# A vision tower on one core: in the expert attention, values laid out by head, their biases added by VectorE, and no gate transposes

## The chip, the cores and the metric

The kernel runs on one core of one Trainium2 chip. The metric is device time in microseconds, the median of three runs: before the change it is 2742.89 us (2742.8 to 2744.47). The core has five engines that run their own instruction streams and wait for one another by semaphores: TensorE (in the profile PE, its weight loads PEld), VectorE (DVE), ScalarE (ACT), GpSimd (POOL) and SyncE (SP, which only issues DMAs here). TensorE writes into PSUM[...]. VectorE and ScalarE empty PSUM into SBUF. Everything is in fp32.

## The reference, cut to what matters

The model is a tokenizer, two transformer layers and, in each, an attention and a feed-forward part. The change touches the feed-forward part of layer 0, which is itself an attention, one for each of 4 experts, 4 chunks of 64 features and 2 heads:

```python
gate = softmax(xn @ router_w.T + router_b, axis=-1)          # 4 gates a token
xc = xn.reshape(B, T, C, DC)                                 # B=128, T=64, C=4, DC=64
qkv = einsum('btcd,ekd->btcek', xc, qkv_w)                   # 4 experts, 2 heads of 32
attn = softmax(einsum('bcehtd,bcehsd->bcehts', q, k) * scale, axis=-1)
y = einsum('bcehts,bcehsd->bcehtd', attn, v)
y = einsum('btced,eod->btceo', y, proj_w) + proj_b           # one bias vector an expert
out = einsum('btceo,bte->btco', y, gate).reshape(B, T, D)
return residual + out @ out_w.T
```

## The kernel before, in words

The stage is the function `expert_attention`. It holds the tokens of all 128 images in SBUF (`h2`) and works on pairs of images: 64 pairs of 2 x 64 = 128 tokens. `Block` does LayerNorm, the transposes of the normalized tokens and the gates for four pairs at once; `Pair` does the attention of one pair.

The weights of values and projection are multiplied together before the loop (`wvp`, L806 to L814), so the "values" of an expert and a head have already been projected to 64 features. The softmax weights are multiplied by the gate (L991, L992 on POOL), so summing over experts and heads in PSUM (`mixed`, L1014) gives the gated output. The projection's bias is brought in apart: before the loop the kernel multiplies the biases by the output matrix (`pb`, `b4`, L819 to L821) and spreads the result by four DMAs over a zeroed tile (`bn`, L823 to L825). For each block the gates are transposed by TensorE (`gates_transpose`, L908) and copied by ScalarE (L911) into one of three zeroed tiles (`gT`, L828), and each pair's `output` adds to its two products with `wo` (L1028) a third one of `gT` with `bn` (L1029). VectorE then adds the sum to `h2` (L1030), and after every fourth pair SP writes four pairs to HBM (L1032).

The order of the work is written out by hand. `with tc.manual_schedule()` keeps each engine's instructions in program order; only what stands before it (the weights, the first blocks' LayerNorm) is ordered by the scheduler. In step p of the loop over pairs three pairs are in flight: scores and softmax of the current pair, the transposes and the mixing of the old one, queries, keys and values of the new one. TensorE's order in a step is: scores (L965), queries and keys of chunk pair 0 (L933), the old pair's second weight transposes (L1001), queries and keys of chunk pair 1, `mixed` (L1014), `values(0)` and `values(1)` (L945), `output` (L1028, L1029), the steps of a block (L908, L874 or L885), and, at the head of the next step, the first weight transposes (L1001). VectorE's order is: maxima and differences of the scores (L977, L978), sums (L984, L985), block steps (statistics L843 and L844 in two of four steps, the logits' steps L892 to L901 in a third), the copies of `values(1)` out of PSUM (L954) and the addition L1030.

`work` holds the steps of the blocks by pair number and place, so the four pairs of a block differ: with p modulo 4, step 0 has a gate transpose and four token transposes on TensorE; step 1 four token transposes, and statistics on VectorE; step 2 the logits, and statistics; step 3 the logits' softmax on VectorE and none of these on TensorE.

All PSUM tiles but the scores come from one pool of four banks with the tag `pq`. A new tile takes the bank that was released longest ago, and its first matmul waits for that bank's last reader.

In `values(fc)`, four 64x64 parts of TensorE's array are used at once: row half `par`, column half `eh`. One call covers two of the four chunks and all 256 columns of `wvp`; its two banks (one for each `par`) are copied by ScalarE for `fc` 0 and by VectorE for `fc` 1.

Of the kernel before, what the change touches and what calls it, by code (L numbers as in the profile page):

```python
# [11 lines left out]
F32 = mybir.dt.float32  # L12
# [7 lines left out]
P = 128  # L20
B = 128
T = 64
D = 256
# [737 lines left out]
def expert_attention(c, hd, normw, wr, br, wqkv, wvT, wproj, bproj, wout):  # L761
# [3 lines left out]
    tc, nc, h2 = c.tc, c.nc, c.h2  # L765
    SCALE = float(1.0 / np.sqrt(np.float32(32)))
    NP = B // 2
    NB = 4
    with (
# [12 lines left out]
        brs = wp.tile([P, 4], F32, name="brs")  # L782
        nc.sync.dma_start(brs, br.partition_broadcast(P))
        w = wp.tile([P, 2 * D], F32, name="w")
        bp2 = wp.tile([P, 4], F32, name="bp2")
        for k in range(2):
            nc.sync.dma_start(w[k * 64 : k * 64 + 64, :], wqkv)
            nc.sync.dma_start(bp2[k * 64 : k * 64 + 64, :], bproj)
        wv = wp.tile([32, 8, 64], F32, name="wv")
        nc.scalar.dma_start(wv, wvT)  # L790
        wpj = wp.tile([32, 8, 64], F32, name="wpj")
# [10 lines left out]
        for k in range(2):  # L802
            for e in range(4):
                for h in range(2):
                    r = (e % 2 * 2 + h) * 64
                    nc.tensor.matmul(  # L806
                        pv[k * 64 : k * 64 + 64, e // 2, r : r + 64],
                        wv[:, e * 2 + h, :],
                        wpj[:, e * 2 + h, :],
                        start=True,  # L810
                        stop=True,
                    )
        wvp = wp.tile([P, 2, D], F32, name="wvp")
        nc.vector.tensor_copy(wvp, pv)  # L814


        pb = psq.tile([4, D], F32, tag="pq", name="pb")
        for fc in range(2):
            nc.tensor.matmul(pb, bp2, wo[:, fc, :], start=(fc == 0), stop=(fc == 1))  # L819
        b4 = wp.tile([4, D], F32, name="b4")  # L820
        nc.vector.tensor_copy(b4, pb)  # L821
        bn = wp.tile([P, NB, D], F32, name="bn")
        nc.gpsimd.memset(bn, 0.0)  # L823
        for n in range(NB):
            nc.sync.dma_start(bn[4 * n : 4 * n + 4, n, :], b4)  # L825
        gTs = [wp.tile([P, P], F32, name=f"gT{k}") for k in range(3)]
        for gT in gTs:
            nc.gpsimd.memset(gT, 0.0)  # L828

        class Block:  # L830

            def __init__(self, p0):
                self.p0, self.gT = p0, gTs[p0 // NB % 3]

            def statistics(self, n0):
                if n0 == 0:
# [63 lines left out]
            def gates(self):  # L903
                nc.gpsimd.tensor_mul(self.gate, self.gate, bcast(self.gm, 2, 4))

            def gates_transpose(self):
                self.pgt = psq.tile([4 * NB, P], F32, tag="pq", name="pgt")
                nc.tensor.transpose(self.pgt, self.gate.rearrange("p n e -> p (n e)"), c.ident)  # L908

            def gates_transposed(self):  # L910
                nc.scalar.copy(self.gT[0 : 4 * NB, :], self.pgt)  # L911

        class Pair:


            def __init__(self, p, blk):
                self.p, self.n, self.blk = p, p % NB, blk
                self.xT = blk.xT[:, :, p % NB, :]
                self.e, self.sm, self.pT = {}, {}, {}

                self.qk = vp.tile([P, 4, 2, 2, P], F32, tag="qk", name="qk", bufs=2)

                self.v = vp.tile([P, 4, 2, D], F32, tag="v", name="v")

            def queries_keys(self, fc):

# [9 lines left out]
                for par in range(2):  # L936
                    nc.scalar.copy(self.qk[:, 2 * fc + par], pq[par])  # L937

            def values(self, fc):
                pv = [psq.tile([P, 2, D], F32, tag="pq", name="pv") for _ in range(2)]  # L940
                for j in range(2):
                    for eh in range(2):
                        for par in range(2):
                            r = slice(par * 64, par * 64 + 64)
                            nc.tensor.matmul(  # L945
                                pv[par][eh * 64 : eh * 64 + 64, j, :],
                                self.xT[r, fc, j * 64 : j * 64 + 64],
                                wvp[r, eh, :],
                                start=True,
                                stop=True,  # L950
                            )
                for par in range(2):
                    copy = nc.scalar.copy if fc == 0 else nc.vector.tensor_copy
                    copy(self.v[:, 2 * fc + par], pv[par])  # L954

            def scores(self):

# [48 lines left out]
            def mixed(self):  # L1006

                pz = psq.tile([P, 2, P], F32, tag="pq", name="pz")
                for fc in range(2):
                    for j in range(2):  # L1010
                        t = slice(j * 64, j * 64 + 64)
                        for r in range(4):
                            for par in range(2):
                                nc.tensor.matmul(  # L1014
                                    pz[par * 64 : par * 64 + 64, fc, t],
                                    self.v[:, 2 * fc + par, j, r * 64 : r * 64 + 64],
                                    self.pT[r // 2][:, r % 2, 2 * fc + par, t],
                                    start=(r == 0),
                                    stop=(r == 3),
                                )  # L1020
                self.z = ep.tile([P, 2, P], F32, tag="z", name="z", bufs=2)
                nc.scalar.copy(self.z, pz)  # L1022

            def output(self):
                p = self.p
                po = psq.tile([P, D], F32, tag="pq", name="po")
                for fc in range(2):
                    nc.tensor.matmul(po, self.z[:, fc], wo[:, fc, :], start=(fc == 0), stop=False)  # L1028
                nc.tensor.matmul(po, self.blk.gT, bn[:, self.n, :], start=False, stop=True)  # L1029
                nc.vector.tensor_add(h2[:, p], h2[:, p], po)  # L1030
                if p % 4 == 3:
                    nc.sync.dma_start(  # L1032
                        hd[2 * p - 6 : 2 * p + 2].rearrange("(n b) t f -> (b t) n f", b=2),
                        h2[:, p - 3 : p + 1],
                    )
# [5 lines left out]
        def at(n, place, f, *a):  # L1041
            key = (n, place) if n >= 0 else "first"
            work.setdefault(key, []).append(lambda: f(*a))

        for b, x in enumerate(blocks):
            n = NB * b
            at(n - 11, "DVE", x.statistics, 0)
            at(n - 10, "DVE", x.statistics, 2)
            at(n - 9, "POOL", x.factors)
            for k in range(NB):  # L1050
                at(n - 8 + k, "POOL", x.normal, k)
            at(n - 4, "PE", x.transpose, 0)
            at(n - 3, "ACT", x.transposed, 0)
            at(n - 3, "PE", x.transpose, 1)
            at(n - 2, "ACT", x.transposed, 1)
            at(n - 2, "PE", x.logits)
            at(n - 1, "DVE", x.logits_less_max)
            at(n - 1, "ACT2", x.exponents)
            at(n - 1, "DVE2", x.sums)
            at(n - 1, "POOL", x.gates)  # L1060
            at(n, "PE", x.gates_transpose)
            at(n + 1, "ACT", x.gates_transposed)

        def do(key):
            for step in work.pop(key, ()):
# [3 lines left out]
        with tc.manual_schedule():  # L1069
            old, cur = None, Pair(0, blocks[0])  # L1070
            for fc in range(2):
                cur.queries_keys(fc)
                cur.values(fc)
            for p in range(NP):
                new = Pair(p + 1, blocks[(p + 1) // NB]) if p + 1 < NP else None
                do((p, "ACT"))
                if old:
                    old.transposed(0)
                cur.scores()
                cur.less_max(0)  # L1080
                cur.less_max(1)
                if new:
                    new.queries_keys(0)
                if old:
                    old.transposed(1)
                cur.exponents(0)
                if new:
                    new.queries_keys(1)
                cur.exponents(1)
                cur.sums(0)  # L1090
                cur.weights(0)
                do((p, "DVE"))
                do((p, "ACT2"))
                cur.sums(1)
                cur.weights(1)
                do((p, "DVE2"))
                do((p, "POOL"))
                if old:
                    old.mixed()
                if new:  # L1100
                    new.values(0)
                    new.values(1)
                if old:
                    old.output()
                do((p, "PE"))
                old, cur = cur, new
            for x in range(2):
                old.transposed(x)
            old.mixed()
            do((NP, "ACT"))  # L1110
            old.output()
        assert not work

# [873 lines left out]
def layout(**i):  # L1987
# [32 lines left out]

    o["wvf"] = w[:, 2].reshape(8, 32, 64).transpose(1, 0, 2)
    o["wproj"] = i["L0_ffn_proj_w"].reshape(4, 64, 2, 32).transpose(3, 0, 2, 1).reshape(32, 8, 64)
    o["bproj"] = i["L0_ffn_proj_b"].T
    o["wout"] = i["L0_ffn_out_w"].T

    q, k, v = (i[f"L1_attn_W{n}"].T.reshape(D, 8, 32).transpose(0, 2, 1).reshape(D, D) for n in "qkv")
# [29 lines left out]
```

## Time and profile before

| what | time or share |
|---|---|
| median of three runs | 2742.89 us |
| the profiled execution's own time | 2744.63 us |
| span of its profile | 2742.5 us, 77026 instructions |
| granted TensorE clock, mean | 0.981 |
| PE / PEld busy | 95% / 63% of the span |
| DVE / ACT / POOL busy | 74% / 59% / 60% |
| values matmuls (L945), 2048 instructions | median 376 ns each |
| values copies (L954), 128 on ACT and 128 on DVE | median 592 and 675 ns |
| gate copies (L911), 16 on ACT | 254 ns each |

The profile is of one execution. In a row of a group stand line, engine, operation, tiles written and read, shape and count; then busy time and the mean duration of one in ns; then the engine's idle time just before these instructions and what ended it. In a timeline a row gives start and length in microseconds of a run of like instructions, and in brackets the idle time before it. A busy TensorE isn't TensorE at its peak, since matmuls overlap; how far apart they start tells more than how long each lasts.

### The profile page before, as it was taken

To read this page: it belongs to the slowest core of one execution; us is meant where nothing else is said; L and a number is where in the kernel's file an instruction comes from. 1 tells how busy PE (TensorE), PEld (TensorE's weight loads), DVE (VectorE), ACT (ScalarE), POOL (GpSimd) and SP (SyncE) were. 2 spreads that over 40 slices of the span, in tenths; PEclk is the share of its full clock that TensorE was granted. 3 is DMA by queue.
4 is the path that set the end of the run, shared out by engine and by line. 5 is a ranking of instruction groups with operands and counts; after the bars stand their busy time and mean duration, and the time that the engine had idled before them with its cause. 6 is when DMAs were issued, how large, how long until landed. Compare 5 with 4: busy or idle time off the path is not lost. (4 is left out here: it accounts for less than half of the span.)

```text
span 2742.5 us, 77026 instructions
## 1 busy us (share of the span) xinstructions
PE 2598.4 (95%) x33309; PEld 1733.3 (63%) x33309; DVE 2027.9 (74%) x3025; ACT 1623.1 (59%) x3414; POOL 1633.7 (60%) x1390
## 2 busy tenths in 40 slices
PE   7989999999999999799999999999699986999997
PEld 4553444444344443588888888888466565888886
DVE  5759999999998989477777777777467776444443
ACT  2228888888888888366656666666355543233332
POOL 3328888888888889656566656553233212454444
PEclk9999999999999999899999999999899998999998
DMA  3000000000000000000000000000333454555554
GB/s 109 32 12 1 2 1 2 2 2 2 1 2 1 2 2 1 12 11 19 11 11 19 11 11 18 11 12 17 96 83 85 100 118 149 179 198 197 184 195 134
DMA packets 138015, 140.83 MB, mean 51 GB/s; under 512 B 107747, under 2 KB 121461, under 8 KB 129984
## 3 DMA queue, kind: packets, MB, share of 16 engines
q1 hardware_dynamic: 126928, 117.95, 14.2%
q0 software_dynamic: 7648, 14.77, 1.7%
q8 instruction: 263, 4.31, 0.6%
q10 hardware_dynamic: 3088, 3.08, 0.4%
q14 instruction: 88, 0.72, 0.1%
HBM read 103.96 MB, written 32.54 MB: 50 GB/s over the span
## 5 line engine op out<-in xcount | busy, mean ns | idle before, releaser
L525 POOL TENSOR_TENSOR m<-q,k 128x1024 f32<-128x1024 f32 x384 | 719.0, 1904 | 31.7 <-PE sc L327 16.3
L517 DVE TENSOR_TENSOR m<-pc,k 128x2048 f32<-128x2048 f32 (+1 forms) x320 | 646.7, 2058 | 0.5 <-ACT q L461 0.5
L327 PE MATMUL sc<-m,wide 128*32 128x512 f32 x4096 | 529.7, 599 | 12.0 <-DVE m L517 7.1
L526 ACT ACTIVATE m<-m 128x1024 f32<-128x1024 f32 x384 | 402.5, 1050 | 5.9 <-POOL m L525 5.4
L327 PEld LDWEIGHTS sc<-m,wide 128*32 128x32 f32 x4096 | 126.6, 109 | 259.6 <-issue 146.2
L535 ACT ACTIVATE m<-k,q 128x64 f32<-128x64 f32 x1024 | 271.0, 339 | 0.8 <-DVE k L408 0.8
L977 DVE TENSOR_REDUCE mx<-sc 128x16 f32<-128x1024 f32 x128 | 156.0, 1219 | 153.2 <-PE sc L965 138.1
L992 POOL TENSOR_TENSOR e<-e,mx 128x1024 f32<-128x1024 f32 x128 | 243.4, 1902 | 10.1 <-POOL mx L991 0.2
L937 ACT COPY qk<-pqk 128x512 f32<-128x512 f32 x256 | 139.0, 604 | 132.2 <-PE pqk L933 132.1
L991 POOL TENSOR_TENSOR mx<-mx,gate 128x16 f32<-128x16 f32 x128 | 27.6, 216 | 314.8 <-ACT z L1022 144.3
L1886 PE MATMUL ph<-xt,w1s 128*128 128x256 f32 x896 | 198.8, 380 | 3.6 <-DVE xt L1877 2.6
L1902 PE MATMUL po<-w2s,hT 128*128 128x256 f32 x896 | 198.0, 379 | 0.0
L1004 ACT COPY pT<-pt 128x512 f32<-128x512 f32 x256 | 138.6, 599 | 99.0 <-PE pt L1001 98.3
L1886 PEld LDWEIGHTS ph<-xt,w1s 128*128 128x128 f32 x896 | 169.8, 190 | 28.2 <-DVE xt L1877 3.2
L1902 PEld LDWEIGHTS po<-w2s,hT 128*128 128x128 f32 x896 | 168.1, 190 | 21.7
L933 PE MATMUL pqk<-xT,w 64*128 64x128 f32 x2048 | 169.6, 289 | 3.7 <-issue 3.5
L978 DVE TENSOR_TENSOR e<-sc,mx 128x1024 f32<-128x1024 f32 x128 | 156.7, 1224 | 4.4
L1920 POOL DMA_INDIRECT out<-y,rout x56 | 56.7, 1013 | 167.8 <-ACT hT L1890 124.8
L933 PEld LDWEIGHTS pqk<-xT,w 64*128 64x128 f32 x2048 | 142.3, 189 | 21.1 <-issue 12.0
L984 DVE TENSOR_REDUCE mx<-e 128x16 f32<-128x1024 f32 x128 | 153.3, 1198 | 2.1 <-ACT e L981 2.0
L1890 ACT ACTIVATE hT<-ph,w1s 128x256 f32<-128x256 f32 x224 | 93.0, 470 | 96.9 <-PE ph L1886 96.9
L1001 PE MATMUL pt<-ident,e 128*128 128x128 f32 x1024 | 141.5, 278 | 5.8 <-POOL e L992 2.8
(308 smaller groups left out, 4958.7 us busy)
## 6 DMA issues: line engine op xcount, KB each, us to landing
w1s<-in_we SPq DMA_DIRECT2D x30, 1028.0 KB, 5.0
w2s<-in_we SPq DMA_DIRECT2D x30, 1024.0 KB, 5.2
hd<-h SPq DMA_DIRECT2D x16, 512.0 KB, 3.4
x<-hd SPq DMA_DIRECT2D x16, 512.0 KB, 5.7
h<-hd SPq DMA_DIRECT2D x4, 2048.0 KB, 12.6
hx<-h SPq DMA_DIRECT2D x4, 2048.0 KB
out<-h SPq DMA_DIRECT2D x4, 2048.0 KB, 20.6
xt<-in_x SPq DMA_DIRECT2D x15, 512.0 KB, 3.5
```

The lines of the kernel that those rows point to most:

```text
L327: nc.tensor.matmul(dst[j : j + 32], wide[:, hf, s : s + 32], part, start=start, stop=stop)
L517: nc.vector.tensor_tensor(m, bcast(self.pq[:, hf, i : i + n], 3, T), k, ALU.max)
L525: nc.gpsimd.tensor_tensor(m, bcast(self.q[:, hf, s : s + 2], 3, T), k, ALU.subtract)
L526: nc.scalar.activation(m, m, AF.Relu)
L535: nc.scalar.activation(self.parts[i, hf][:, q], self.blk.k[:, hf, i], AF.Relu, bias=self.q[:, hf, i - NB // 2, q : q + 1], scale=-1.0,)
L933: nc.tensor.matmul(pq[par][:, k, eh, :], w[r, f : f + P], self.xT[r, fc], start=True, stop=True)
L977: nc.vector.tensor_reduce(mx, sc, AX.X, ALU.max)
L978: nc.vector.tensor_sub(e, sc, bcast(mx, 2, T))
L984: nc.vector.tensor_reduce(self.sm[x], self.e[x], AX.X, ALU.add)
L992: nc.gpsimd.tensor_mul(e, e, bcast(sm, 2, T))
L1886: nc.tensor.matmul(ph[:, j], self.w1[:, w0 : w0 + P], self.xt[:, fc], start=(fc == 0), stop=(fc == 1))
L1902: nc.tensor.matmul(po, self.hT[:, f, r * P : r * P + P], self.w2[:, f, :], start=(f == 0), stop=(f == 7))
```

## The change

The bias of expert e is moved into the values. Each row of softmax weights sums to one and is then multiplied by the gate, so a bias added to the values of one head, for every source token, comes out as gate times bias, which is what the reference adds. It is added to the second head alone.

To let one engine do so for a whole bank, the values are laid out by head: the columns of `wvp` are put in order of head and then expert, `values(h)` computes head h for all four chunks, with 128 columns a matmul where there were 256, and twice as many matmuls. ScalarE copies head 0; VectorE empties head 1 with an addition of the tile `bv` (128 x 128, the biases of two experts on each half of the partitions, broadcast over the chunks) where it copied. `bv` is loaded by two broadcasting DMAs. The tile `v` is indexed by `par`, head, chunk and expert. The product of `gT` with `bn`, the gate transposes and copies, and the making of `bn` and `gT` ahead of the loop are gone. The host gives the biases untransposed.

```diff
         w = wp.tile([P, 2 * D], F32, name="w")
-        bp2 = wp.tile([P, 4], F32, name="bp2")
+        bv = wp.tile([P, P], F32, name="bv")
         for k in range(2):
             nc.sync.dma_start(w[k * 64 : k * 64 + 64, :], wqkv)
-            nc.sync.dma_start(bp2[k * 64 : k * 64 + 64, :], bproj)
+            nc.sync.dma_start(
+                bv[k * 64 : k * 64 + 64, :],
+                bproj[2 * k : 2 * k + 2].rearrange("e o -> (e o)").partition_broadcast(64),
+            )
...
-                    r = (e % 2 * 2 + h) * 64
+                    r = (h * 2 + e % 2) * 64
...
-        pb = psq.tile([4, D], F32, tag="pq", name="pb")
-        for fc in range(2):
-            nc.tensor.matmul(pb, bp2, wo[:, fc, :], start=(fc == 0), stop=(fc == 1))
-        b4 = wp.tile([4, D], F32, name="b4")
-        nc.vector.tensor_copy(b4, pb)
-        bn = wp.tile([P, NB, D], F32, name="bn")
-        nc.gpsimd.memset(bn, 0.0)
-        for n in range(NB):
-            nc.sync.dma_start(bn[4 * n : 4 * n + 4, n, :], b4)
-        gTs = [wp.tile([P, P], F32, name=f"gT{k}") for k in range(3)]
-        for gT in gTs:
-            nc.gpsimd.memset(gT, 0.0)
...
-            def gates_transpose(self):
-                self.pgt = psq.tile([4 * NB, P], F32, tag="pq", name="pgt")
-                nc.tensor.transpose(self.pgt, self.gate.rearrange("p n e -> p (n e)"), c.ident)
-
-            def gates_transposed(self):
-                nc.scalar.copy(self.gT[0 : 4 * NB, :], self.pgt)
...
-                self.v = vp.tile([P, 4, 2, D], F32, tag="v", name="v")
+                self.v = vp.tile([P, 2, 2, 4, P], F32, tag="v", name="v")
...
-            def values(self, fc):
-                pv = [psq.tile([P, 2, D], F32, tag="pq", name="pv") for _ in range(2)]
-                for j in range(2):
-                    for eh in range(2):
-                        for par in range(2):
-                            r = slice(par * 64, par * 64 + 64)
-                            nc.tensor.matmul(
-                                pv[par][eh * 64 : eh * 64 + 64, j, :],
-                                self.xT[r, fc, j * 64 : j * 64 + 64],
-                                wvp[r, eh, :],
-                                start=True,
-                                stop=True,
-                            )
+            def values(self, h):
+
+                pv = [psq.tile([P, 4, P], F32, tag="pq", name="pv") for _ in range(2)]
+                for fc in range(2):
+                    for j in range(2):
+                        for eh in range(2):
+                            for par in range(2):
+                                r = slice(par * 64, par * 64 + 64)
+                                nc.tensor.matmul(
+                                    pv[par][eh * 64 : eh * 64 + 64, 2 * fc + j, :],
+                                    self.xT[r, fc, j * 64 : j * 64 + 64],
+                                    wvp[r, eh, h * P : h * P + P],
+                                    start=True,
+                                    stop=True,
+                                )
                 for par in range(2):
-                    copy = nc.scalar.copy if fc == 0 else nc.vector.tensor_copy
-                    copy(self.v[:, 2 * fc + par], pv[par])
+                    if h == 0:
+                        nc.scalar.copy(self.v[:, par, 0], pv[par])
+                    else:
+                        nc.vector.tensor_add(self.v[:, par, 1], pv[par], bcast(bv, 1, 4))
...
-                                    self.v[:, 2 * fc + par, j, r * 64 : r * 64 + 64],
+                                    self.v[:, par, r % 2, 2 * fc + j, r // 2 * 64 : r // 2 * 64 + 64],
...
-                    nc.tensor.matmul(po, self.z[:, fc], wo[:, fc, :], start=(fc == 0), stop=False)
-                nc.tensor.matmul(po, self.blk.gT, bn[:, self.n, :], start=False, stop=True)
+                    nc.tensor.matmul(po, self.z[:, fc], wo[:, fc, :], start=(fc == 0), stop=(fc == 1))
```

More of the change, by code (lines that the diff above doesn't have):

```diff
@@ L814, in expert_attention @@
         nc.vector.tensor_copy(wvp, pv)
-        pb = psq.tile([4, D], F32, tag="pq", name="pb")
-        for fc in range(2):
-            nc.tensor.matmul(pb, bp2, wo[:, fc, :], start=(fc == 0), stop=(fc == 1))
-        b4 = wp.tile([4, D], F32, name="b4")
-        nc.vector.tensor_copy(b4, pb)
-        bn = wp.tile([P, NB, D], F32, name="bn")
-        nc.gpsimd.memset(bn, 0.0)
-        for n in range(NB):
-            nc.sync.dma_start(bn[4 * n : 4 * n + 4, n, :], b4)
-        gTs = [wp.tile([P, P], F32, name=f"gT{k}") for k in range(3)]
-        for gT in gTs:
-            nc.gpsimd.memset(gT, 0.0)
         class Block:
             def __init__(self, p0):
-                self.p0, self.gT = p0, gTs[p0 // NB % 3]
+                self.p0 = p0
             def statistics(self, n0):
@@ L1060, in expert_attention @@
             at(n - 1, "POOL", x.gates)
-            at(n, "PE", x.gates_transpose)
-            at(n + 1, "ACT", x.gates_transposed)
         def do(key):
@@ L1109, in expert_attention @@
             old.mixed()
-            do((NP, "ACT"))
             old.output()
@@ L2022, in layout @@
     o["wproj"] = i["L0_ffn_proj_w"].reshape(4, 64, 2, 32).transpose(3, 0, 2, 1).reshape(32, 8, 64)
-    o["bproj"] = i["L0_ffn_proj_b"].T
+    o["bproj"] = i["L0_ffn_proj_b"]
     o["wout"] = i["L0_ffn_out_w"].T
```

## The prediction

> **What bounds the kernel now.** I read the page first. Its part 4, the chain that ended last, holds only the kernel's last fraction of a per cent, so it says nothing here. The busy shares by window do: in the expert attention (about 1128 to 1942 us of the span) every full window looks like this one, whose columns are busy us of PE, weight loads, DVE, ACT and POOL.
>
> ```profile
> 1500.00:1600.00 100.00, 99.53 (x2299) 83.79 (x2305) 77.81 (x114) 62.55 (x114) 60.71 (x69) 1.00 0.05 14
> ```
>
> PE looks like the bound, but a busy PE includes matmuls that wait in its pipeline, so I went on to the groups by shape, 1300 to 1700 us (32 pairs, 33 at the edges; duration is the latency of one, not its spacing).
>
> ```profile
> L945 PE MATMUL pv<-wvp,xT 64*64 64x256 f32 x1024 | 71.2, 388 | 0.1
> ...
> L954 DVE COPY v<-pv 128x512 f32<-128x512 f32 x64 | 39.6, 660 | 0.5 <-PE pv L945 0.3
> ...
> L1029 PE MATMUL po<-bn,gT 128*128 128x256 f32 x64 | 19.0, 379 | 0.0
> ...
> L1030 DVE TENSOR_TENSOR h<-h,po 128x256 f32<-128x256 f32 x32 | 13.3, 416 | 3.2 <-PE po L1029 3.2
> ...
> L908 PE MATMUL pgt<-ident,gate 128*16 128x128 f32 x8 | 2.2, 272 | 0.0
> ```
>
> Counts per pair are 32 values instructions and 2 bias instructions (each fp32 matmul is two instructions). What a step occupies comes from starts, in the timeline of PE. This is pair 32, whose scores began at 1537.91:
>
> ```profile
> 1544.91 2.10 PE L945 MATMUL pv<-wvp,xT 64*64 64x256 f32 x32
> 1546.93 1.13 PE L1028 MATMUL po<-wo,z 128*128 128x256 f32 x4
> 1547.90 0.59 PE L1029 MATMUL po<-bn,gT 128*128 128x256 f32 x2
> 1548.33 0.27 PE L908 MATMUL pgt<-ident,gate 128*16 128x128 f32 x1
> 1548.44 0.60 PE L874 MATMUL ptx<-ident,xn 128*128 128x128 f32 x4
> 1548.88 1.04 PE L1001 MATMUL pt<-ident,e 128*128 128x128 f32 x8
> 1549.85 0.37 PE L965 MATMUL sc<-qk 32*64 32x64 f32 x16
> ```
>
> PE runs without a gap from the output product to the next scores: bias 0.43 us (1547.90 to 1548.33), gate transpose 0.11. The next pair, 33, is different:
>
> ```profile
> 1560.17 1.22 DVE L954 COPY v<-pv 128x512 f32<-128x512 f32 x2
> 1560.27 0.60 PE L874 MATMUL ptx<-ident,xn 128*128 128x128 f32 x4
> ...
> 1560.63 1.90 POOL L992 TENSOR_TENSOR e<-e,mx 128x1024 f32<-128x1024 f32 x1
> ...
> 1560.92 0.95 PEld L1001 LDWEIGHTS pt<-ident,e 128*128 128x128 f32 x8 [0.29 <-issue]
> 1560.95 1.16 PE L1001 MATMUL pt<-ident,e 128*128 128x128 f32 x8
> 1561.31 0.41 DVE L1030 TENSOR_TENSOR h<-h,po 128x256 f32<-128x256 f32 x1
> ```
>
> The 0.29 us is labelled "issue", but PE's sequencer waited there for DVE's first values copy (its semaphore moved at 1560.82) because the transposes take the PSUM buffer it empties; the second half waited likewise for 1561.41.
>
> I name pairs by their number modulo 4 and measure score start to score start. In undisturbed groups they take 11.94 (0), 12.19 (1), 13.13 (2) and 12.36 (3), 49.62 us together. Pair kind 1: DVE has two LayerNorm statistics steps (about 1.1 us) ahead of its copies and sets the end. Kind 2 has statistics too, but 16 logits instructions on PE (1.71 us) come first. Kind 0 is PE alone. In kind 3 the values stall 0.49 us for DVE's gate step, early; after that PE runs on.
>
> [...] Here 256 columns step at 215.5 ns and 128 columns at 109[...]. [...] the first values matmul lasts 427 against 376 ns[...]. [...] four values matmuls start within 20 ns here. [...] The new add has one from PSUM. In the lines above L1030, of that same form, takes 0.41 beside POOL's 1.90 us step, its usual 416 ns: no exclusion.
>
> **The change, part by part.**
> Bias product gone: 2 x 0.2155 = 0.43 us of PE a pair. Gate transpose gone: 0.11 us in kind 0; its ScalarE copy (254 ns, L911) has idle time of ScalarE before and after it and nobody waits for it, so it counts nothing.
>
> Values by head: 64 instructions of 128 columns for 32 of 256, four at a time. Before, a half is 4 steps of 215.5 = 0.862 plus the 0.052 first load; after, 8 steps of 109 to 112 (the transposes' and L933's spacing) = 0.87 to 0.90 plus 0.052. [...] The second half starts only when ScalarE has emptied z (8.0 us after the scores' start; the first half ends at about 7.95), so one half counts: +0.03 us a pair. Bounds of the step: 109 (all streaming) to 215.5 (no gain from the shorter operand).
>
> DVE's copy becomes an add of PSUM and a broadcast SBUF tile. No row has it at 512 columns. [...] the rows of 256 (416) and 1024 (1224) interpolate to 685. The two copies last 628 and 675, starting 545 apart; adds should start 610 apart (1024 columns: 1.15 between starts, less 0.53). So the second buffer is free 0.07 us later. Bounds: 0 to 0.15.
>
> By kind, in us:
> - 0: -0.43 - 0.11 + 0.03 = -0.51. Transposes would start 10.46 after the scores. What is late next: POOL's first weighted scores, ready at 10.20, and DVE's first copy, at 9.8; neither holds.
> - 1: PE comes 0.4 earlier to the wait for DVE, and the gain turns into wait. DVE's chain starts from the scores and is 0.07 longer: +0.07.
> - 2: -0.43 + 0.03 = -0.40; DVE's first buffer is free at 10.9, the transposes move from 12.13 to 11.73.
> - 3: -0.40; the buffers for its transposes are free at 9.97 and about 10.8, they start at 11.0.
> Group: -1.24. Fourteen groups (pairs 4 to 59): -17.4. Pairs 1 to 3: -1.2. The last four: -0.9, for there POOL's weighted scores (10.3) stop the earlier transposes, and the very last output gains 0.43. Five pairs of kind 1 (5, 45, 49, 53, 57) have a PE pause of about 1 us without a wait in view, so PE and not DVE ends them: another 0.45 each, -2.2.
>
> Ahead of the loop: POOL's memsets of bn (0.95) and gT (0.49) go; its factors could then start when the fourth statistics are ready (1114.33, not 1114.68), and POOL's chain leads to the first scores: -0.3. The pb product, its copy and SP's four 0.6 us DMA issues are behind nothing that waits: SP's next issue, the first write of results, comes over 50 us later. The bias load stays two DMAs of 64 rows on SP; it has 20 us until the first add. I take those at zero; without cover the two DMAs cost their difference in landing, under 1 us once.
>
> The added instructions, 60 a pair on about 560, are 10% more to fetch. If the pauses above are fetches, their total (nine groups exceed 49.62 by 5.6 us together) grows by 0.6. Bounds: 0 to 5, and they can fall elsewhere.
>
> Sum: -17.4 - 1.2 - 0.9 - 2.2 - 0.3 + 0.6 = -21.4. The profiled execution took 2744.63, its span 2742.5; so 2723.2 for it. The runs' median, 2742.89, is 1.74 lower: 2721.5.
>
> **Rivals.**
> A. PE bounds every pair: 64 x 0.40 + 16 x 0.11 + 0.3 = 27.7 us, 2715. It needs DVE's wait in kind 1 to vanish; the trace shows that wait in nine of the fourteen pairs 5 to 57 of that kind. Chance 0.09.
> B. The gain is half swallowed: with PE earlier, POOL's weighted scores (0.26 us from kind 0's new start), ScalarE's chain or fetch pauses hold kinds 0, 2 or 3. Half of -21.4: 2732. For it, margins of a quarter microsecond; against, 1 us of slack in kind 2. Chance 0.11.
> C. Slower: the step of four 64x64 tiles doesn't shrink with its columns, as for the scores, whose eight tiles of 64 columns step at 96 ns, not 55. It decides at a step of (1.724 + 0.43)/16 = 0.135 us where both halves count, 0.16 where one does. At 0.2155, 16 steps take 3.45 us for 1.88: +1.6 a pair, less 0.43: 2742.9 + 64 x 1.15 = 2816. Against: the scores' rate is 12 ns per load and matmul, so four need 48 ns, under 109. Chance 0.10.
> D. POOL's L992 does hold back DVE's adds, by about 0.8 us: kind 1 +0.8, kind 0 -0.35, kind 2 -0.4, kind 3 -0.2, so the group stays and so does the time, 2741. Against: L1030 above. Chance 0.05.
>
> **Numbers.** My forecast has 0.65, at 2721.5; its own range is 2717 to 2727. About 0.2% (5.5 us) is what a measurement of this kernel can tell from no change. Faster: 0.65 + 0.09 + B's 0.11 less 0.01 = 0.84. Same: D and that part of B, 0.06. Slower: C, 0.10. The 8-in-10 range takes in A and most of B, and leaves out C and D: 2712 to 2734.
>
> **What would show it.** Right: in the timeline no product from bn; 64 values instructions a pair stepping at about 0.11 in fours; pairs of 11.43, 12.26, 12.73 and 11.96 us; kind 1 with 0.6 us of wait on DVE ahead of its transposes; DVE's adds about 685 ns. Wrong: values over 2.3 us with no stall inside them (C); kind 1 as much shorter as the others (A); transposes waiting for POOL in kind 0 (B); adds over 0.9 us beside POOL's L992 (D).

## The result, and the profile after

The changed kernel takes 2725.68 us (median of four runs, 2722.33 to 2727.22), the kernel before, on the same chip, 2742.85 us (four runs, 2742.14 to 2744.47). The ratio is 0.9935, with a 95% interval of 0.9918 to 0.9952: 0.65% faster. The profiled execution took 2725.85 us, its span is 2724.2 us, so 18.3 us shorter than the span before.

First the busy shares by window, columns as in the prediction (busy us of PE, weight loads, DVE, ACT and POOL, granted clock, DMA share, GB/s):

```profile
1500.00:1600.00 100.00, 98.07 (x2528) 86.99 (x2528) 80.29 (x119) 62.40 (x113) 62.96 (x71) 1.00 0.05 14
```

PE still looks full, with 10% more instructions in the same 100 us. Then the groups by shape, 1300 to 1700 us, of the changed kernel:

```profile
L932 PE MATMUL pv<-wvp,xT 64*64 64x128 f32 x2112 | 72.1, 275 | 0.5
...
L990 PE MATMUL pt<-ident,e 128*128 128x128 f32 x520 | 72.5, 279 | 4.5 <-DVE v L943 3.1 <-issue 0.3
...
L943 DVE TENSOR_TENSOR v<-pv,bv 128x512 f32<-128x512 f32 x66 | 41.0, 662 | 0.4
...
L1018 DVE TENSOR_TENSOR h<-h,po 128x256 f32<-128x256 f32 x33 | 13.5, 410 | 0.0
```

There are 64 values instructions a pair where there were 32, and no product from `bn`. DVE's addition out of PSUM lasts 662 ns on average, in the same view in which the copy it replaces lasted 660. The 3.2 us that DVE's last addition had waited for the bias product are gone (0.0 in the row of L1018); 3.1 us of wait for DVE's values stand now ahead of PE's transposes (L990). The timeline of PE for pair 32 (kind 0), whose scores began at 1527.72:

```profile
1534.72 2.11 PE L932 MATMUL pv<-wvp,xT 64*64 64x128 f32 x64
1536.76 1.13 PE L1017 MATMUL po<-wo,z 128*128 128x256 f32 x4
1537.73 0.60 PE L865 MATMUL ptx<-ident,xn 128*128 128x128 f32 x4
1538.16 1.04 PE L990 MATMUL pt<-ident,e 128*128 128x128 f32 x8
1539.13 1.59 PE L954 MATMUL sc<-qk 32*64 32x64 f32 x128
```

The values start 7.00 us after the scores and the output product 9.04, as before (9.02); read one by one, the values matmuls step at 0.109 us in fours after a first step of 0.16. The token transposes follow the output product with nothing between, and the next scores come 11.41 us after the last. And the timeline of all engines at the end of pair 33 (kind 1), rows left out:

```profile
1549.13 0.60 PE L865 MATMUL ptx<-ident,xn 128*128 128x128 f32 x4
...
1549.46 1.22 DVE L943 TENSOR_TENSOR v<-pv,bv 128x512 f32<-128x512 f32 x2
...
1549.91 1.90 POOL L981 TENSOR_TENSOR e<-e,mx 128x1024 f32<-128x1024 f32 x1
...
1550.23 1.16 PE L990 MATMUL pt<-ident,e 128*128 128x128 f32 x8 [0.50 <-DVE v L943]
1550.60 0.41 DVE L1018 TENSOR_TENSOR h<-h,po 128x256 f32<-128x256 f32 x1
```

PE waits 0.50 us for DVE's first addition and the pair is no shorter. DVE's two additions take 1.22 us together beside POOL's 1.90 us step, as the copies did.

The time from score start to score start, in undisturbed groups, and what the prediction had for it:

| kind of pair | before | predicted | after |
|---|---|---|---|
| 0 | 11.94 | 11.43 | 11.41 |
| 1 | 12.19 | 12.26 | 12.19 |
| 2 | 13.13 | 12.73 | 12.71 |
| 3 | 12.36 | 11.96 | 11.94 |
| four pairs | 49.62 | 48.38 | 48.25 |

So every undisturbed group gains 1.37 us. That alone is 19.2 us in the fourteen groups, more than the whole span gained. Most of the rest went into pauses of PE. Here is the timeline of all engines around the scores of pair 22 (kind 2) in the changed kernel, rows left out:

```profile
1403.88 1.50 PE L954 MATMUL sc<-qk 32*64 32x64 f32 x117
...
1406.39 0.22 PEld L954 LDWEIGHTS sc<-qk 32*64 32x64 f32 x11 [1.16 <-issue]
1406.40 0.36 PE L954 MATMUL sc<-qk 32*64 32x64 f32 x11 [1.02 <-issue]
```

In the middle of a run of like matmuls, for which no wait is shown, PE does nothing for 1.02 us. The DMA view of the same kernel from 1403 to 1407 us (queue, kind: packets, MB, share) has one packet in it:

```profile
q8 instruction: 1, 0.02, 2.1%
```

It is a packet of 16,384 bytes in the instruction queue, from 1403.80 to 1405.16 us; PE goes on at 1406.40. The kernel before has such pauses too, at other places; its timeline of PE in pair 45 (the window cuts the start of the first row):

```profile
1700.29 1.40 PE L965 MATMUL sc<-qk 32*64 32x64 f32 x109
1702.49 0.34 PE L965 MATMUL sc<-qk 32*64 32x64 f32 x8 [0.80 <-issue]
1702.76 1.16 PE L933 MATMUL pqk<-xT,w 64*128 64x128 f32 x16
```

I call the excess of a kernel the time by which its pairs 4 to 59 exceed the undisturbed length of their kind. It is 6.3 us before and 8.8 after. (Pairs 53 and 57 have no statistics ahead of VectorE's values steps and are measured against the shorter length that this leaves: 11.83 before, 11.41 after.) The difference of the spans in parts:

| part | predicted, us | measured, us |
|---|---|---|
| before the stage | 0 | -1.1 |
| head of the stage, to the first scores | -0.3 | -0.5 |
| pairs 0 to 3 | -1.2 | -1.4 |
| kinds 0, 2 and 3 of pairs 4 to 59, undisturbed lengths | -18.3 | -19.2 |
| nine pairs of kind 1 | +0.6 | 0.0 |
| the other five of kind 1 (5, 45, 49, 53, 57) | -1.9 | -3.3 |
| pauses elsewhere in pairs 4 to 59 | +0.6 | +4.9 |
| pairs 60 to 63, to the last write's issue | -0.9 | +0.3 |
| from there to the end | 0 | +1.8 |
| sum | -21.4 | -18.5 (spans: -18.3) |

The predicted column splits the prediction's terms anew, with the same sum: its -1.24 a group is -1.31 for kinds 0, 2 and 3 and +0.07 for kind 1. The first row and the last but one, which the change doesn't touch, are chance of two executions: a second profile of the changed kernel, at the end of the experiments, reaches the first scores 1.2 us later than this one, and takes from the last write's issue to the end 800.4 us instead of 802.6 (before: 800.8).

### The profile page after: what moved, and what is told of

Its sections match the earlier page's. It is cut to its first block, busy times and chain, and to the rows that moved or that the text cites. A ratio compares the mean times of both kernels' runs of the same rounds, so it can differ in the third digit from the quotient of the medians.

```text
span 2724.2 us, 80786 instructions
## 1 busy us (share of the span) xinstructions
PE 2574.9 (95%) x35209; PEld 1749.1 (64%) x35209; DVE 2023.0 (74%) x3024; ACT 1619.3 (59%) x3398; POOL 1632.4 (60%) x1386
## 5 line engine op out<-in xcount | busy, mean ns | idle before, releaser
L981 POOL TENSOR_TENSOR e<-e,mx 128x1024 f32<-128x1024 f32 x128 | 243.5, 1903 | 10.1 <-POOL mx L980 0.2
L990 PE MATMUL pt<-ident,e 128*128 128x128 f32 x1024 | 144.0, 281 | 11.1 <-DVE v L943 5.1
## 6 DMA issues: line engine op xcount, KB each, us to landing
out<-h SPq DMA_DIRECT2D x4, 2048.0 KB, 20.5
```

Of the source, the lines that this page charges most:

```text
L981: nc.gpsimd.tensor_mul(e, e, bcast(sm, 2, T))
```

## The experiments

**One half of the change: the products gone.** The theory was that the removed matmuls are the gain and the new layout costs nothing; the rival, that the layout of the values by head takes some of it back. The bias product, the gate transposes and their copies are gone, and the values are computed by chunk and copied, as before. No projection bias is added anywhere.

```diff
 (against the changed kernel)
-                    r = (h * 2 + e % 2) * 64
+                    r = (e % 2 * 2 + h) * 64
...
-            def values(self, h):
+            def values(self, fc):
+                pv = [psq.tile([P, 2, D], F32, tag="pq", name="pv") for _ in range(2)]
...
+                                wvp[r, eh, :],
...
+                    copy = nc.scalar.copy if fc == 0 else nc.vector.tensor_copy
+                    copy(self.v[:, 2 * fc + par], pv[par])
```

> The bias product and the gate transposes are taken out, and the values stay by chunk with plain copies; the projection's bias is left out of the computation. My theory (the values by head cost next to nothing themselves: 0.02 us a pair): undisturbed pairs of kinds 0 to 3 take 11.39, 12.19, 12.69 and 11.92 us, as in the changed kernel, and with 60 instructions a pair fewer on TensorE there are fewer pauses; 2719 to 2724 us. Rival (the values by head cost 0.1 us a pair or more, hidden in a sum that came out nearly right): kinds 0, 2 and 3 are 0.1 us shorter than in the changed kernel, 11.31, 12.61, 11.84, and the time is below 2719.

Measured: 2724.11 us (2722.17 to 2727.42), ratio 0.9922 (0.9908 to 0.9935). The pairs are 11.40, 12.18, 12.70 and 11.93: 0.01 below the changed kernel's each. Its timeline of PE at the same place of pair 32:

```profile
1541.67 1.13 PE L1013 MATMUL po<-wo,z 128*128 128x256 f32 x4
1542.64 0.60 PE L865 MATMUL ptx<-ident,xn 128*128 128x128 f32 x4
1543.08 1.04 PE L986 MATMUL pt<-ident,e 128*128 128x128 f32 x8
```

Spacings of 0.97 and 0.44 us, the changed kernel's to the hundredth. So the removal is the gain, and the layout costs 0.01 us a pair. The other half of the expectation fell. This kernel has the fewest PE instructions of all, 2264 in four pairs (before 2283, changed 2520), and an excess of 9.2 us, in fifteen pairs. So the pauses don't grow with the number of instructions to fetch.

**The other half: by head alone.** The kernel before with the values by head, VectorE copying, and the bias product and gate transposes kept.

```diff
 (against the kernel before)
-                    r = (e % 2 * 2 + h) * 64
+                    r = (h * 2 + e % 2) * 64
...
+                    if h == 0:
+                        nc.scalar.copy(self.v[:, par, 0], pv[par])
+                    else:
+                        nc.vector.tensor_copy(self.v[:, par, 1], pv[par])
```

> The kernel before with the values by head alone: copies on both engines, bias product and gate transposes kept. My theory: kinds 0 to 3 take 11.96, 12.19, 13.15 and 12.38 us; with 64 instructions a pair more on TensorE the pauses grow by 1 to 4 us; 2743 to 2749 us. Rival (more instructions cost no time by themselves, the pauses of the changed kernel were chance): within 1.5 us of the kernel before, the summed pauses as there (6.3 us).

Measured: 2747.54 us (2744.98 to 2750.46, thirteen runs), ratio 1.001 (1.0001 to 1.0018). The pairs are 11.95, 12.19, 13.14 and 12.37, before plus 0.01 or nothing. The excess is 9.7 us, 3.4 more than before, but pair 57 alone holds 2.8 of it, and not by pauses alone: besides a pause of 1.5 us in its scores, it has a stretch of half clock (granted 0.5), from 1855.6 to 1859.0. The spans differ by 3.5 us, and this doesn't measure the layout either, since pairs 0 to 2 lost 1.7 us in another half-clock stretch and the first scores came 2.0 us earlier. So in undisturbed pairs the layout costs 0.03 us a group, 0.4 us in all; what it costs by pauses that fall elsewhere, one profile can't tell.

**Where the pauses stand.** I numbered PE's records in the trace of each kernel. A pause without a wait comes at a number that leaves 193 when divided by 256. The changed kernel's 70,698 records of PE make 276.2 blocks of 256, and the instruction queue moved 278 packets, each of 16,384 bytes; before, 66,913 records make 261.4, and it moved 263. So I took one packet for one block of PE's instructions. If a pause belongs to a block, moving the blocks against the pairs must move the pauses, and nothing else. So 32 tiny matmuls (with their loads 128 instructions, half a block) went into idle time of PE ahead of the stage.

```diff
-            c.busy(psq.tile([P, 8, T], F32, tag="pq", name="idle"), blocks[-1].k[:, 0, 0:8], 5)
+            pe = psq.tile([P, 8, T], F32, tag="pq", name="idle")
+            c.busy(pe, blocks[-1].k[:, 0, 0:8], 5)
+            for _ in range(32):
+                nc.tensor.matmul(pe[0:4, 0, 0:4], c.ident[:, 0:4], blocks[-1].k[:, 0, 0, 0:4], start=True, stop=True)
```

> The changed kernel with 32 tiny matmuls (128 TensorE instructions) more in an idle stretch of TensorE ahead of the stage. My theory (the pauses without a wait are instruction fetches, one for every 256 instructions): all pauses still stand at one place modulo 256 in TensorE's instruction stream, but half a fetch further on in the program, so they fall on other pairs than 6, 11, 13, 20, 22, 24, 26, 36, 44, 46, 50 and 52; the pair lengths outside them do not change; the time moves by up to 4 us either way, 2721 to 2730. Rival (the pauses belong to a place in the step, for instance beside the writes of results): they stay at those pairs and the time stays within 1 us of the changed kernel, 2725 to 2727.

Measured: 2731.22 us (2729.4 to 2732.11), ratio 0.9949 (0.9936 to 0.9963). The undisturbed lengths are the changed kernel's. The pauses stand at the same number, 193 of 256, and have moved to other pairs: those of 11, 13, 20, 22, 24, 37, 44, 46, 50 and 52 are gone, and 8, 10, 12, 14, 23, 25, 29, 34, 38, 40 and 58 have them. The excess is 8.9 us, against 8.8 without the shift: pairs 4 to 59 took 682.77 us, the changed kernel's 682.71. The time is above the expected range. In the profiled execution (2729.4 us) pairs 0 and 1 fell into a stretch of half clock (granted 0.5, 1150.3 to 1153.7 us) and took 12.54 and 12.78 us for 11.27 and 12.12, the last pairs took 0.5 us more, and the first scores came 0.6 us later. Half clock in pairs 0 and 1 is not the shift's doing: three other profiles have it at 1146 us, two of them of kernels without the tiny matmuls. For the four runs without a trace the difference stays open.

**Undoing the wait in kind 1.** The theory was that VectorE's statistics hold back the additions and with them PE's transposes. Here they come after the additions, and nothing is left out.

```diff
-            at(n - 11, "DVE", x.statistics, 0)
-            at(n - 10, "DVE", x.statistics, 2)
+            at(n - 11, "DVE3", x.statistics, 0)
+            at(n - 10, "DVE3", x.statistics, 2)
...
                     new.values(1)
+                do((p, "DVE3"))
```

> The changed kernel, with VectorE's LayerNorm statistics put behind its additions to the values. My theory (kind 1 is ended by VectorE, whose statistics hold up the additions that free the banks): kind 1 falls from 12.19 to 11.4 us, the others stay at 11.41, 12.71 and 11.94; twelve or thirteen pairs by 0.78 us make 9 to 10 us, 2714 to 2718. Rival (something else ends kind 1, POOL's weighted scores or TensorE itself): kind 1 stays at 12.1 or more, 2723 to 2728.

Measured: 2715.17 us (2713.88 to 2716.68), ratio 0.9891 (0.9876 to 0.9906). Kind 1 takes 11.41 us, as kind 0; the others are unchanged. The timeline of DVE in a pair of kind 1:

```profile
1494.02 0.25 DVE L974 RECIPROCAL mx<-mx 128x16 f32<-128x16 f32 x1
1494.19 1.23 DVE L943 TENSOR_TENSOR v<-pv,bv 128x512 f32<-128x512 f32 x2
1495.34 0.42 DVE L834 BATCH_NORM_STATS2 st<-h 128x6 f32<-128x256 f32 x1
```

The additions start straight after the sums. So the statistics are the bound of kind 1, and its lost gain comes back when they move: 0.78 us in each of twelve pairs, 9.4 us. Against that, the excess rose by 1.7 us, to 10.5.

**The stall in kind 3.** There the values had waited for VectorE's gate step, which stood behind the scores' maxima. It now stands ahead of the first.

```diff
-            at(n - 1, "DVE", x.logits_less_max)
+            at(n - 1, "DVE0", x.logits_less_max)
...
                 cur.scores()
+                do((p, "DVE0"))
```

> The changed kernel, with VectorE's three gate steps on the logits (which free the logits' bank) moved from behind the sums to ahead of the first maximum of the scores, where VectorE has idle time. My theory: kind 3 no longer waits 0.49 us for that bank inside its values and ends, as POOL's weighted scores allow, at 11.35 to 11.45 us instead of 11.94; the other kinds stay at 11.41, 12.19 and 12.71; fifteen pairs by 0.5 us make 7 to 8 us, 2716 to 2720. Rival (the three steps only move VectorE's chain back by their 0.5 us, and kind 3 ends by that chain): kind 3 stays at 11.9 or more, 2724 to 2728.

Measured: 2716.74 us (2715.65 to 2718.13), ratio 0.9902 (0.9886 to 0.9917). Kind 3 takes 11.28 us instead of 11.94, a little more gain than expected. The timeline of DVE and, after it, that of PE, both of this kernel:

```profile
1512.00 0.41 DVE L1018 TENSOR_TENSOR h<-h,po 128x256 f32<-128x256 f32 x1
1512.57 0.18 DVE L883 TENSOR_TENSOR pg<-pg,brs 128x16 f32<-128x16 f32 x1 [0.15 <-PE pg L876]
...
1514.95 1.23 DVE L966 TENSOR_REDUCE mx<-sc 128x16 f32<-128x1024 f32 x1 [1.79 <-PE sc L954]
```

```profile
1518.30 2.08 PE L1003 MATMUL pz<-pT,v 128*64 128x64 f32 x64
1520.32 2.21 PE L932 MATMUL pv<-wvp,xT 64*64 64x128 f32 x64
```

DVE does the step while it would wait for the scores anyway (1.79 us of idle time are left), and the values follow the mixing without a stall. The excess is about 11 us.

**Both moves together.** The edits of the last two experiments in one kernel, to see whether the gains add up.

> The changed kernel with the statistics behind the additions and the gate steps ahead of the maxima, both. My theory: kinds of 11.41, 11.41, 12.71 and 11.4 us; 2704 to 2710. Rival (with both, POOL's weighted scores of the first half, ready 10.3 us after the scores' start, hold kinds 1 and 3, or the pauses grow): 2710 to 2715.

Measured: 2705.63 us (2703.26 to 2706.99), ratio 0.986 (0.9845 to 0.9875). The pairs are 11.41, 11.41, 12.71 and 11.28, so the gains add; the excess is 10.2 us. It is 20 us below the changed kernel and 38.0 below the kernel before in its own comparison (2743.59): the best version here.

**Blocks aligned with the pairs.** In the changed kernel four pairs are 2520 instructions, so the place of a block's end drifts by 40 from group to group and runs through the whole pair. Ten tiny matmuls in kind 1 (40 instructions), where PE waits for DVE anyway, make 2560, ten blocks. Every group then has its block ends at the same places: first at 46, 188, 34 and 152 instructions after the start of the scores of kinds 0 to 3, where pairs had seldom been longer so far. The next ends follow 256 instructions later, for kinds 0 and 2 at 302 and 290. There the changed kernel does pause (0.2 to 0.5 us at four ends between 286 and 308 in its first profile), but those pairs are hardly longer.

```diff
             def transpose(self, fc):
                 self.pt = psq.tile([P, NB, P], F32, tag="pq", name="ptx")
+                if fc == 1 and self.p0 >= 8:
+                    for _ in range(10):
+                        nc.tensor.matmul(
+                            self.pt[0:4, 0, 0:4], c.ident[:, 0:4], c.ident[:, 0:4], start=True, stop=True
+                        )
```

> The changed kernel with ten tiny matmuls (40 TensorE instructions) more in each pair of kind 1 from pair 5 on, ahead of its token transposes, where TensorE waits for VectorE anyway. Four pairs then hold 2560 instructions, ten fetches of 256 exactly, so in every group the fetch boundaries stand at the same places, 46, 188, 34 and 152 instructions after the start of the scores of kinds 0 to 3; in the changed kernel no pause stood at 34 to 188, and all but one at 190 to 275. My theory (a pause comes where a fetch's 256 instructions are mostly those of the scores): the summed excess of pairs 4 to 59 falls from 8.8 us to under 3, the pair lengths stay 11.41, 12.19, 12.71, 11.94; 2718 to 2722. Rival (pauses come with the traffic of the DMA queues at their own times, the place in the stream only shows when one strikes): the excess stays at 6 to 10 us; 2724 to 2729.

Measured: 2721.48 us (2718.93 to 2723.79), ratio 0.992 (0.9906 to 0.9933). The timeline of PE in pair 33:

```profile
1544.72 1.13 PE L1022 MATMUL po<-wo,z 128*128 128x256 f32 x4
1545.78 0.65 PE L866 MATMUL ptx<-ident 128*4 128x4 f32 x20
1546.36 0.66 PE L870 MATMUL ptx<-ident,xn 128*128 128x128 f32 x4
1546.85 1.09 PE L995 MATMUL pt<-ident,e 128*128 128x128 f32 x8
```

The added matmuls take 0.58 us of PE and kind 1 is still 12.19: the wait for DVE covers them. In pairs 53 and 57, which have no such wait, they cost 0.72 us each. The excess is 5.4 us with these two, 3.9 without: less than half of the changed kernel's 8.8, though not the less than 3 that I expected. The repeats below show what this means.

**The last two again, side by side.** The changed kernel itself, and the aligned one, on one chip.

> The changed kernel again, to stand beside the aligned one on one chip. Its pauses fell at the same pairs in every kernel whose TensorE stream before the pair is the same, so I expect them at pairs 22, 26, 46 and 50 again, with 8 to 11 us in all for pairs 4 to 59, and 2723 to 2728 us. Rival (the pauses are chance of an execution): other pairs, 5 to 12 us in all.

> The kernel with aligned fetches again. If alignment is what saved time there, it is 3 to 5 us below the changed kernel beside it, and its excess without the two padded pairs 53 and 57 is under 5 us. Rival (chips and days differ): within 1.5 us of the changed kernel.

Measured: 2725.75 us (2723.85 to 2726.64) for the changed kernel, ratio 0.9936 (0.9922 to 0.995), and 2720.97 us (2717.19 to 2725.22) for the aligned one, ratio 0.9919 (0.9906 to 0.9933). The excess is 8.4 and 5.2 us (3.7 without the two uncovered pairs). The changed kernel's large pauses (22, 26, 46, 50) came at the same pairs again. The medians differ by 4.8 us, by about 4 in the runs above. The ranges of each two overlap, but eight of the ten executions of the aligned kernel are below all nine of the changed one, so the gain in time is there.

The pauses themselves did not become fewer. Against the spacing of the same instructions where no block ends, pairs 4 to 59 of the aligned kernel pause at 20 and 25 block ends (its two profiles), by 9.6 and 10.8 us in all; those of the changed kernel at 17 and 15, by 11.5 and 11.2 us. What changed is where: 18 and 23 of the aligned kernel's stand at 290 and 302, in the transposes behind the scores. Here is PE in pair 16, first in the changed kernel (scores from 1332.81), then in the aligned one (scores from 1332.32), both from these repeats, rows left out:

```profile
1335.43 1.09 PE L990 MATMUL pt<-ident,e 128*128 128x128 f32 x8
1336.45 1.41 PE L918 MATMUL pqk<-xT,w 64*128 64x128 f32 x16
...
1341.85 1.13 PE L1017 MATMUL po<-wo,z 128*128 128x256 f32 x4
```

```profile
1334.93 0.87 PE L995 MATMUL pt<-ident,e 128*128 128x128 f32 x6
1335.99 0.38 PE L995 MATMUL pt<-ident,e 128*128 128x128 f32 x2 [0.19 <-issue]
1336.30 1.16 PE L923 MATMUL pqk<-xT,w 64*128 64x128 f32 x16
...
1341.35 1.13 PE L1022 MATMUL po<-wo,z 128*128 128x256 f32 x4
```

The transposes lose 0.35 us to the pause, and the output product starts 9.03 us after the scores all the same, as in the changed kernel (9.04): queries, keys and values, which otherwise stretch by waits, give the time back. A pause inside the scores has nothing of the kind behind it: in pair 46 of the changed kernel it made 1.26 us of pause into 1.31 us of excess. So the place of the blocks sets what a pause costs. A kernel with as many added matmuls and its block ends inside the scores, which would test this from the other side, was not run.

## Why the prediction was right, and where its sum was off

The forecast was 2721.5 us, with 2712 to 2734 as its range and 2717 to 2727 as its own. The measured 2725.68 lies in both: the kernel is faster, by 17.2 us where 21.4 were forecast. The mechanism was right, pair by pair, in the undisturbed groups. The sum is off by the pauses; its other errors, up and down, nearly cancel, and that is luck.

- **What the matmuls were worth.** Kinds 0, 2 and 3 became 0.53, 0.42 and 0.42 us shorter, where 0.51, 0.40 and 0.40 were worked out. The values by head took 0.01 us a pair instead of 0.03, since their step is 109 ns, the lower bound of the estimate.
- **VectorE's addition.** It was taken at 685 ns, with the second buffer free 0.07 us later. It lasts as long as the copy (662 against 660 ns in the groups; the medians over the kernel are 678 and 675), and the two of a pair start a median 546 ns apart, the copies 545, where 610 was expected; so kind 1 kept its 12.19 us. This term's lower bound of 0 was the right one. With the first point it makes the group's gain 1.37 and not 1.24, 1.8 us over fourteen groups.
- **Kind 1 swallows its gain.** Predicted as about 0.6 us of wait on DVE; the row shows 0.50, and moving the statistics away gave the 0.78 us back.
- **The pauses: the term that was off.** The prediction left the pauses where the trace of before had them, in five pairs of kind 1, took -2.2 us for these and +0.6 for 10% more to fetch. The five pairs did better than that (-3.3 for -1.9 with their share of the 0.07), but not by 0.45 each: 45, 49, 53 and 57 lost the excess that their pauses had made (2.4 us together), 53 and 57, which have no statistics ahead of VectorE's values steps and so are ended by PE, gained 0.42 each besides, and pair 5 gained nothing. But the pauses came back in other pairs, mostly of kinds 0 and 2, where no wait of DVE's hides any of them: +4.9 us for +0.6. Together that is +1.6 for -1.3, 2.9 us, as much as the whole sum is off by. The bound "0 to 5, and they can fall elsewhere" held it. The reckoning by the number of instructions was wrong, as the kernel with the fewest instructions and an excess of 9.2 us shows; what counts is which instructions stand at a block's end, and what waits follow them.
- **The tail and the stage after.** The last four pairs were to gain 0.9 us. The first three of them did gain 0.6, and the last lost 0.85. The next stage, linear attention, counted as unchanged, and the way from its first load to the end became 2.1 us longer. The windows of the changed kernel show what is different there; the last columns are the granted clock, DMA share and GB/s:

```profile
1911.50:1918.30 6.80, 5.77 (x50) 5.02 (x52) 0.16 (x1) 2.34 (x4) 2.87 (x3) 0.50 0.00 0
2177.70:2181.10 3.40, 3.40 (x10) 1.24 (x8) 2.17 (x5) 0.00 (x0) 0.00 (x0) 0.50 1.38 218
2187.90:2191.40 3.50, 3.50 (x8) 1.38 (x6) 3.36 (x3) 0.40 (x1) 0.00 (x0) 0.51 0.00 0
```

  In the kernel before, the last pair runs at full clock to its end (1.00 from 1922 to 1929 us), and so it does in the kernel by head alone, which keeps the bias product; all nine profiles without the product have a half-clock stretch of 3.4 or 6.8 us in it. Linear attention of the kernel before has no half-clock stretch at the two later places (1.00 from 2196 to 2200 and from 2206 to 2210 us). The half-clock stretches of these two kernels' profiles, but for the one that runs to the end of each, are 3.4, 6.8, 10.2, 17.1 or 20.5 us long at a granted clock of 0.5, with 1.0 between them; what brings one on was not shown. The two later stretches are not the change's doing: the second profile of the changed kernel has neither, and takes 796.5 us from the load to the end, where the first took 798.8 and the kernel before 796.7. Over the eleven profiles, the four with both stretches take 798.6 to 799.2 us, the seven others 795.6 to 797.6. So these 2 us come and go between executions of one kernel.

Of the rivals, A (PE bounds every pair) fell on kind 1's 12.19 us and its wait. B (half swallowed by POOL or ScalarE) fell: kinds 0, 2 and 3 have the whole gain, and no transposes wait for POOL in pair 32; the loss that did occur came from fetch pauses, which B had named. C (the step of 64x64 tiles doesn't shrink) fell on the step of 0.109 us, against 0.135 at which it would have decided. D (POOL holds back the additions) fell on 662 ns beside POOL's L981.

## What to carry to other kernels

Taking small matmuls off a full TensorE gave 0.42 to 0.53 us a pair here, about their spacing (0.43 for the product, 0.11 for the transpose), in kinds 0, 2 and 3, where no wait for another engine came after them, and nothing in kind 1 (12.19 us before and after), which VectorE ended. Where another engine ends the step, move that engine's deferrable work behind the step that TensorE waits for; with the gate steps moved out of kind 3's way too, that gave as much again here as the change itself (20 us). An edit that changes the number of TensorE's instructions also moves the later block ends, and the pauses moved with them here: half a block more took them from ten pairs to eleven others. A pause cost its length where no wait followed that could give it back (1.26 us of pause and 1.31 us of excess in pair 46). The excess was 5.2 to about 11 us in these kernels, so look at the "issue" gaps and number the instructions before reading a difference of 0.1 to 0.2%.

## What the runs showed of the hardware

In these runs TensorE waited for its instructions, by up to 1.6 us at a time. The instruction queue moved packets of 16,384 bytes, about one for every 256 of PE's records, and the pauses without a wait came only at every 256th. Most block ends show none. In the eleven profiles, pairs 4 to 59 hold 1496 block ends. The spacing at each was set against the median spacing at the same instruction of like pairs where no block ends (for the aligned kernel, whose ends always fall at the same places, of the changed one). Of the 405 ends that lie 160 to 319 instructions behind the start of the scores, 182 (45%) have a pause of 0.15 to 1.6 us; of the other 1091, none. Between 224 and 287 it is 87 of 119. The 256 scores' instructions go through in 1.6 us, and 256 of the 2520 of four pairs in 4.9 us on average (48.25 for all), so a block that is mostly scores is used up about three times as fast as the average.

The times of the packets say that PE waits for them there. Counted in order they pair off with the blocks (278 packets for 277 blocks in the changed kernel), so each end has its packet. At no end did PE go on earlier than 1.2 us after its packet had ended. At all 182 pauses it went on 1.20 to 1.65 us after; at 1262 of the 1314 ends without a pause, it came later than that anyway. A packet begins a median 0.7 us after PE has entered the block before (nine in ten between -0.1 and 1.6) and lasts 0.9 to 1.7 us. From typical values of these, 0.7 + 1.0 + 1.3, an estimate: a block that takes PE under about 3 us is likely to be followed by a pause. What sets the moment at which a packet begins, no run here settles. Two excesses of 0.3 us, in pairs 6 and 36 of nearly every kernel, don't stand at a block's end; in the changed kernel PE's weight loads wait there for ScalarE (0.24 and 0.28 us), and why it is late wasn't followed up.
